# A fused attention and FP8 block on one core: later chunks prepared in pairs at other places, and entries' keys copied ahead of the divisions

## The chip, the cores and the metric

The kernel runs on one core of one Trainium2 chip. The metric is the device time of one execution in microseconds (us). The engines are TensorE (PE, matrix multiplication; PEld its weight loads), VectorE (DVE), ScalarE (ACT), GpSimd (POOL) and SyncE (SP), which here does nothing but issue DMAs. Each engine works through its own list of instructions in order and waits on semaphores for what others have to finish first.

## The reference, cut to what matters

The input `x` has 4 rows of 1024 tokens with 512 features. It is layer-normalized, and then three things are added: `x` itself, an attention layer, and a product with FP8-rounded operands.

```python
xn = layernorm(x)
out = x + attention(xn) + fp8_matmul(xn, input2)

# attention, per batch row, 16 heads of 128
q   = rope(rmsnorm(xn @ Wq + bq))
w   = softmax over groups of 4 tokens of (xn @ Wcmp + bcmp)
entries = sum over each group of w * xn          # 256 entries a row
ck  = rope(rmsnorm(entries @ Wk + bk)); cv = entries @ Wv + bv
sc  = q . ck, causal; the best 8 entries, softmax over them, times cv
lk  = rope(rmsnorm(xn @ Wlk + blk));  lv = xn @ Wlv + blv
local = softmax(q . lk over this and the previous 128 tokens) @ lv
attention = (sparse + local) / 2 @ Wo + bo
```

## The kernel before

**Chunks and units.** The tokens are cut into `NT` = 32 chunks of 128, eight to a batch row, numbered `t` = 0 to 31. A chunk has `NU` = 8 units `u`, each of two heads: unit `n` is `8 t + u`. One loop (L1012) goes over the units. In step `s` it issues, for several units at once, the pieces of a software pipeline: scores and softmax of unit `s`, queries of `s + 3`, normalization of the queries and keys of `s + 2`, values of `s - 1`, context and output of `s - 2`. The order in which these calls stand in the loop is the order on every engine; nothing reorders them.

For unit `s`, TensorE makes the scores (L750 for the previous 128 tokens, L757 for its own, L760 for the entries, out of `ckT`). `weigh` (L762) masks them and finds the best 8 on VectorE, then ScalarE takes the exponentials (L810, L818). `settle` (L821) removes what was not chosen and makes the reciprocals on VectorE, and `divide` (L838) multiplies on ScalarE (L843). `turn` (L854) transposes blocks of the probabilities on VectorE (L861), stores them to DRAM (`pr`, L869), and `fetch` (L898) brings them back transposed as `probT` (L903). `values` (L908), one step later, multiplies them with the values (L920). The first chunk and the last units do these transpositions on TensorE instead. The more entries there are, the wider the rows: chunks 1 to 3 of a batch row have three blocks of 128 a head, chunks 4 to 7 four.

**Preparing a later chunk.** `chunk_prep(t)` (L348) is a generator. It normalizes the tokens, transposes them by blocks on VectorE into `xb`, stores that to DRAM, and makes the weighted sums of four tokens, `few`, which lies in the same buffer as `xb`, and stores that to DRAM as `pooled`. The loop runs it on to a named step in given units (`FIRST_HALF`, `SECOND_HALF`, L991 to L992). A table `ready` (L998) says which chunks are prepared in which chunk. Where it names two, the second, `extra`, runs by `FIRST_HALF_MORE` and `SECOND_HALF_MORE` (L993 to L994) in units 2 to 5, and its `x` lies in a buffer of the tag `scratch`. That tag has two buffers; `xb` and the temporaries `qv` and `qm` of `chunk_eight` (L572, the FP8 part, which starts in unit 5 of every chunk) use it too.

The `pooled` store of chunks 0 to 7 is issued where the sums are made (L440); later ones are put into a list `stores`, which is issued near the end of a step (L1078), behind the fetches.

**Making entries.** `chunk_entries(g, n)` (L504) makes keys and values of entries from the pooled sums of the first `n` chunks of group `g` (`GC` = 4 chunks, 128 entries). A table `made` (L1000) says in which chunk this runs. It loads the sums in unit 4, multiplies on TensorE in unit 5 (L533, tile `ep`), normalizes and rotates on VectorE in units 5 and 6, and in unit 7 transposes the keys on TensorE (L568, tile `cp`) and copies them on ScalarE to `ckT` (L569). Unit 0 of the next chunk is the first to read them (L760). The generator is in the list `running`; `steps()` (L968) takes every generator there one step further, and is called twice in a step: once after `divide` and `turn` (L1052), once after the queries' squares (L1063). So the transposition and the copy of unit 7 stand at the first of these calls, behind the divisions on ScalarE.

## Time and profile before

| what | value |
|---|---|
| time, median of 3 runs | 2648.14 us (2648.01 to 2652.9) |
| the profiled execution's own time | 2649.72 us |
| its span, first to last instruction | 2647.9 us |
| mean granted TensorE clock | 0.999 of full speed |
| TensorE matmuls busy | 2607.9 us, 98% |
| VectorE busy | 2214.4 us, 84% |
| ScalarE busy | 1389.3 us, 52% |
| GpSimd busy | 783.9 us, 30% |
| DMA | 422.20 MB, 159 GB/s on the mean |

The page of the profile begins with the busy shares. Its second part cuts the span into 40 slices and gives each engine's busy share in tenths:

```profile
PE   8999999999999999999999999999999999999998
PEld 4666667676666666766766666666676666676776
DVE  6888888888888888888988888888888888877886
ACT  3545545555555555555555555555555555555554
```

The busy times of matmuls are modelled ends, so a digit 9 may still hold short waits. A list of waits names, for an engine, the line that waited, what ended its wait, the total time, how often, and the longest. A timeline gives start and duration of single instructions, or of several in a row that are alike, and in brackets the idle time before them with what ended it.

### The profile page before, as it was taken

The numbers are of one execution on the slowest core, as the hardware profiler recorded it, in microseconds if no ns is written. First come the engines' busy times: TensorE is split into PE (matmuls) and PEld (weight loads), VectorE is DVE, ScalarE is ACT, GpSimd is POOL, SyncE is SP. The second block draws the span as 40 slices with busy tenths as digits, with TensorE's granted clock in tenths as the row PEclk, the third lists the DMA queues.
The fourth block names the chain that finished last, engine by engine and source line by source line (L and its number), as shares of the span: only waits on it lengthen the run. The fifth ranks groups of instructions, "written<-read, shape, count | busy, mean of one in ns | idle before, by whom it ended". The sixth has DMA issues, their size and how long they took to land.

```text
span 2647.9 us, 46825 instructions
## 1 busy us (share of the span) xinstructions
PE 2607.9 (98%) x11844; PEld 1784.6 (67%) x11879; DVE 2214.4 (84%) x8381; ACT 1389.3 (52%) x5560; POOL 783.9 (30%) x1128
## 2 busy tenths in 40 slices
PE   8999999999999999999999999999999999999998
PEld 4666667676666666766766666666676666676776
DVE  6888888888888888888988888888888888877886
ACT  3545545555555555555555555555555555555554
POOL 3522333223332223232233222232323332322222
PEclk9999999999999999999999999999999999999999
DMA  8456556666655555666655556665665555566554
GB/s 252 113 155 160 149 139 177 178 166 161 165 142 157 158 150 162 165 175 175 162 156 147 155 148 159 172 165 159 174 180 144 149 147 152 150 167 172 158 152 111
DMA packets 722157, 422.20 MB, mean 159 GB/s; under 512 B 395728, under 2 KB 671457, under 8 KB 721889
## 3 DMA queue, kind: packets, MB, share of 16 engines
q1 hardware_dynamic: 721280, 418.80, 58.8%
q8 instruction: 97, 1.59, 0.3%
q14 instruction: 172, 1.40, 0.2%
q10 hardware_dynamic: 608, 0.41, 0.1%
HBM read 225.80 MB, written 193.20 MB: 158 GB/s over the span
## 4 chain that ended last, share of the span: by engine, by line
PE 83%; DVE 8%; ACT 3%; DMA 3%; SPq 1%; issue 1%; POOL 0%; DVEq 0%; ACTq 0%; POOLq 0%
PE qp L602 28%; PE op L953 14%; PE vp L708 14%; PE cp L920 13%; PE sc L760 5%; PE sc L757 4%; PE sc L750 4%; ACT prob L843 1%; ACT prob L810 1%; PE fp L584 1%; DVE sc L782 1%; DVE taken L808 1%; DVE probB L861 1%; PE ep L533 1%; ACT prob L818 1%
## 5 line engine op out<-in xcount | busy, mean ns | idle before, releaser
L602 PE MATMUL qp<-wqk,xnT 128*128 128x512 f32 x1552 | 711.0, 594 | 2.7 <-DMA wqk<-in_L_attn_Wlk_dram 2.7
L810 ACT ACTIVATE prob<-sc,neg 128x256 f32<-128x256 f32 (+1 forms) x512 | 235.6, 460 | 777.2 <-DVE taken L808 749.0
L602 PEld LDWEIGHTS qp<-wqk,xnT 128*128 128x128 f32 x1552 | 295.6, 191 | 372.2 <-issue 369.5
L843 ACT ACTIVATE prob<-prob,tot 128x256 f32<-128x256 f32 (+7 forms) x1024 | 382.0, 443 | 297.1 <-DVE tot L836 297.1
L708 PEld LDWEIGHTS vp<-wlv,xnT 128*128 128x128 f32 x2048 | 389.0, 190 | 161.2 <-issue 116.0
L953 PE MATMUL op<-wo,cT 128*128 128x512 f32 x1024 | 481.6, 593 | 2.8 <-ACT cT L935 2.8
L708 PE MATMUL vp<-wlv,xnT 128*128 128x256 f32 x2048 | 483.6, 379 | 0.0
L334 POOL TENSOR_TENSOR rb<-th,cs 128x256 f32<-128x256 f32 x256 | 203.3, 794 | 740.6 <-DVE th L630 733.6
L782 DVE CUSTOM_DVE_ANT_0 sc<-sc,mask_b 128x256 f32<-128x256 f32 (+1 forms) x512 | 211.5, 413 | 178.1 <-PE sc L760 168.0
L953 PEld LDWEIGHTS op<-wo,cT 128*128 128x128 f32 x1024 | 193.6, 190 | 228.4 <-issue 183.9
L861 DVE STREAM_TRANSPOSE probB<-prob 128x512 f32<-128x512 f32 (+2 forms) x490 | 305.7, 629 | 11.4 <-ACT prob L843 0.4
L312 POOL TENSOR_SCALAR r<-ss 128x4 f32<-128x4 f32 x256 | 61.0, 238 | 846.4 <-ACT junk L318 843.7
L920 PE MATMUL cp<-probT,lv 128*128 128x128 f32 x1920 | 298.7, 275 | 6.6 <-DMA probT<-pr 5.4
L318 ACT ACTIVATE junk<-qp 128x128 bf16<-128x128 f32 x1024 | 278.0, 272 | 29.7 <-PE qp L610 5.3
L920 PEld LDWEIGHTS cp<-probT,lv 128*128 128x128 f32 x1920 | 273.1, 191 | 24.7 <-issue 11.7
L630 DVE SCALAR_TENSOR_TENSOR th<-qp,r,norm_w 128x128 f32<-128x128 f32 x1024 | 286.1, 342 | 1.9 <-POOL r L313 1.6
L313 POOL TENSOR_TENSOR r<-r,nhalf 128x4 f32<-128x4 f32 x256 | 265.3, 1037 | 21.3
L826 DVE SCALAR_TENSOR_TENSOR prob<-taken,prob 128x128 f32<-128x128 bf16 (+7 forms) x512 | 187.2, 366 | 97.4 <-ACT prob L818 93.5
L602 PE MATMUL qp<-wqk,xone 128*128 128x512 f32 x496 | 258.3, 602 | 1.2 <-DMA xone<-xb_dram 1.2
L920 PE MATMUL cp<-probT,cv 128*128 128x128 f32 x1536 | 255.1, 275 | 0.0
L760 PE MATMUL sc<-ckT,qT 128*128 128x96 f32 (+7 forms) x1024 | 226.7, 303 | 6.9 <-ACT ckT L569 6.9
L920 PEld LDWEIGHTS cp<-probT,cv 128*128 128x128 f32 x1536 | 212.7, 192 | 0.0
(141 smaller groups left out, 3663.3 us busy)
## 6 DMA issues: line engine op xcount, KB each, us to landing
pr<-probB SPq DMA_DIRECT2D x125, 512.0 KB
probT<-pr SPq DMA_DIRECT2D x500, 128.0 KB
qk<-thb SPq DMA_DIRECT2D x992, 64.0 KB
pr<-probB SPq DMA_DIRECT2D x96, 384.0 KB
probT<-pr SPq DMA_DIRECT2D x384, 96.0 KB
qT<-qk SPq DMA_DIRECT2D x248, 128.0 KB
lkT<-qk SPq DMA_DIRECT2D x248, 128.0 KB
x_norm<-_attn_hidden_states_dram SPq DMA_DIRECT2D x32, 256.0 KB
```

Source lines behind the costliest of these rows:

```text
L313: nc.gpsimd.tensor_tensor(r, r, nhalf[: ss.shape[0], 0:n], ALU.pow)
L318: nc.scalar.activation(junk[: src.shape[0]], src, AF.Square, accum_out=acc)
L602: nc.tensor.matmul(qp, xnT[:, k, :] if k or not t else xone, wqk_sb[u][:, k, :], start=(k == 0), stop=(t > 0 and k == KK - 1),)
L630: nc.vector.scalar_tensor_tensor(th[:, i, :], qp[:, ts(i, D)], r[:, i : i + 1], norm_w[:, i // 2, :], ALU.mult, ALU.mult,)
L708: nc.tensor.matmul(vp[:, 0:256], xnT[:, k, :], wlv_sb[u][:, k, :], start=(k == 0), stop=(k == KK - 1),)
L760: nc.tensor.matmul(sc[:, spa], q, ckT[:, 0:m], start=True, stop=True)
L782: nc.vector.tensor_tensor_reduce(sc[h][:, loc], sc[h][:, loc], mask_b[:, loc], -1.0, TAKEN, ALU.add, ALU.min, neg[h][0],)
L810: nc.scalar.activation(probs[h][:, loc], sc[h][:, loc], AF.Exp, bias=neg[h][0], scale=-1.0, accum_out=tot[:, h, 0:1],)
L843: nc.scalar.mul(probs[h][:, cols], probs[h][:, cols], tot[:, h, part : part + 1])
L861: nc.vector.transpose(pb[:, :, ds(h * g, g), :], prob[:, parts[0] * P : (parts[-1] + 1) * P].rearrange("p (g b i) -> p b g i", b=NB, i=BLK),)
L920: nc.tensor.matmul(blocks(cp[:, h, :]), v, probT[:, :, h * len(parts) + i - parts[0], :], start=(i == parts[0]), stop=(i == parts[-1]),)
L953: nc.tensor.matmul(op, cT[:, h, :], wo_sb[u][:, h, :], start=(u == 0 and h == 0), stop=(u == NU - 1 and h == 1),)
```

## The change

It has three parts.

- `ready` and `made` change. Two chunks are prepared in chunks 2, 4 and 6 instead of 1, 2 and 3: chunk 1 prepares chunk 2, chunk 2 the chunks 3 and 4, chunk 3 chunk 5, chunk 4 the chunks 6 and 7, chunk 5 chunk 8, chunk 6 the chunks 9 and 10, chunk 7 chunk 11. From chunk 8 on nothing changes. The number of chunks with two stays three. Entries are made in chunks 0, 1, 2, 3 and 5 of the first batch row instead of 0, 1, 2, 3 and 4, and in chunk 3 from two chunks of the group instead of three; those in chunk 7 and later stay.
- The `pooled` store of chunks 8 to 11 is issued where the sums are made, too.
- In unit 7 of a chunk that makes entries, the generator is taken out of `running`. Its transposition is issued behind `queries` of that step, and its copy to `ckT` behind `settle` and ahead of `divide`. No instruction of TensorE lies between the old and the new place of the transposition, so only ScalarE's order changes: the copy comes ahead of the four divisions.

```diff
@@ chunk_prep
-        if t < 2 * GC:
+        if t < 3 * GC:
             nc.sync.dma_start(pooled[g][i], few)
         else:
             stores.append((pooled[g][i], few))
@@ chunk_entries
         nc.tensor.transpose(cp[:, 0:P], ck[:, 0, :], ident)
+        yield "turned"
         nc.scalar.copy(ckT[:, ts(half, P)], cp[:, 0:P])
         yield "A7"
@@ the tables
-    ready = {-1: [0], 0: [1], 1: [2, 3], 2: [4, 5], 3: [6, 7]}
-    ready.update({t: [t + GC] for t in range(GC, NT - GC)})
-    made = {0: (0, 2), 1: (0, 3), 2: (0, GC), 3: (1, 3), 4: (1, GC)}
+    ready = {-1: [0], 0: [1], 1: [2], 2: [3, 4], 3: [5], 4: [6, 7], 5: [8], 6: [9, 10], 7: [11]}
+    ready.update({t: [t + GC] for t in range(2 * GC, NT - GC)})
+    made = {0: (0, 2), 1: (0, 3), 2: (0, GC), 3: (1, 2), 5: (1, GC)}
     made.update({t: ((t + 1) // GC, GC) for t in range(2 * GC - 1, NT - 1, GC)})
@@ the loop over units
         for_unit(s + 3, (queries,))
+        if u == 7 and t in made:
+            running.remove(begun)
+            until(begun, "turned")
         if s < 0:
...
         for_unit(s, (settle,))
+        if u == 7 and t in made:
+            until(begun, "A7")
         for_unit(s, (divide,))
```

## The prediction, made before the changed kernel was run

> **What bounds the kernel.** I read first the page's busy shares: TensorE 98%, VectorE 84%, ScalarE 52%. So only TensorE's stalls can be won or lost. Then I cut the span at the first own-chunk score matmul (L757) of each chunk, from TensorE's timeline, and asked for busy times by these stretches. Chunks are numbered from 0, eight to a batch row; those below are 1 to 7, then 10, 11, 12 and 14.

> ```profile
> core 0: us, PE busy (x) PEld busy (x) DVE busy (x) ACT busy (x) POOL busy (x), PEclk, DMA share, GB/s
> 117.47:202.44 84.97, 81.06 (x362) 54.12 (x362) 70.72 (x278) 39.44 (x167) 27.12 (x39) 1.00 0.54 144
> 202.44:288.21 85.77, 81.40 (x366) 54.73 (x366) 70.55 (x283) 43.12 (x178) 25.18 (x42) 1.00 0.57 151
> 288.21:374.49 86.28, 81.63 (x367) 54.80 (x366) 71.14 (x279) 43.95 (x178) 25.13 (x40) 1.00 0.57 149
> 374.49:460.18 85.69, 83.84 (x395) 58.66 (x394) 73.00 (x273) 46.52 (x181) 24.54 (x38) 1.00 0.63 166
> 460.18:543.13 82.95, 82.90 (x389) 57.86 (x389) 71.89 (x261) 44.07 (x172) 23.78 (x33) 1.00 0.64 171
> 543.13:627.21 84.08, 83.99 (x389) 58.62 (x389) 74.07 (x261) 44.71 (x172) 24.29 (x33) 1.00 0.63 168
> 627.21:713.95 86.74, 86.69 (x396) 60.51 (x396) 75.53 (x264) 45.24 (x172) 25.71 (x36) 1.00 0.65 167
> ...
> 864.17:942.10 77.93, 77.88 (x357) 52.85 (x357) 64.85 (x260) 41.87 (x171) 22.26 (x33) 1.00 0.56 155
> 942.10:1021.99 79.89, 79.84 (x367) 54.85 (x366) 66.34 (x265) 42.87 (x174) 23.82 (x36) 1.00 0.57 155
> 1021.99:1103.63 81.64, 81.59 (x386) 56.55 (x385) 70.48 (x262) 43.92 (x174) 23.22 (x33) 1.00 0.63 170
> ...
> 1186.58:1271.22 84.64, 84.00 (x390) 58.65 (x389) 73.91 (x260) 44.53 (x172) 24.33 (x33) 1.00 0.63 167
> ```

> The first column is the length of the stretch. Chunks 10, 11 and 12 do what 2, 3 and 4 do, but prepare one later chunk each and (11 alone) make entries: there TensorE idles 0.05 us. They are my rows for a clean chunk. Making entries costs 11 against 10 only 1.95 us, of which 1.85 are the ep matmuls in unit 5. Chunks 1 to 3, which prepare two and make entries, lose 4 to 5 us each. The waits of VectorE and TensorE in chunks 1 to 3 say how:

> ```profile
> DVE qm_x L285 <- DMA pooled<-xb: 9.8, 3, 3.5
> DVE xb L375 <- DMA pooled<-xb: 7.9, 3, 2.7
> ...
> PE cp L920 <- DMA probT<-pr: 4.5, 5, 1.2
> PE sc L760 <- ACT ckT L569: 2.9, 2, 1.6
> ```

> (Columns: total us, times, longest.) Each pair stops VectorE twice, on the two buffers of the tag `scratch`: in unit 3 the second chunk's xb needs the buffer of the first until its pooled store has landed, in unit 5 chunk_eight's qm needs that of the second. VectorE's timeline of chunk 2 has both:

> ```profile
> 244.17 0.65 DVE L429 TENSOR_REDUCE xb<-x_norm 128x128 f32<-128x512 f32 x1
> ...
> 247.88 0.71 DVE L375 STREAM_TRANSPOSE xb<-x_norm 128x512 f32<-128x512 f32 x1 [2.61 <-DMA pooled<-xb]
> ...
> 271.74 0.43 DVE L285 TENSOR_SCALAR qm_x<-qv_x 128x512 uint32<-128x512 uint32 x1 [3.36 <-DMA pooled<-xb]
> ```

> **How a pair becomes TensorE time.** weigh (L782) starts at 235.40 in unit 3 of chunk 2 and at 272.54 in unit 6: 37.14 us for three units. Three clean units of chunk 10 take 3 x 9.635 = 28.90, so VectorE falls 8.24 behind. TensorE's ep matmuls fill 1.85 of it. The rest, 6.39, reaches TensorE through turn, its store and fetch, values. From the end of turn (L861) to the first L920 a clean unit of chunk 10 has 9.22 us; where it waited, in unit 6 of chunk 2 (turn ended 279.66, L920 began 286.56), the path took 6.90. So 2.32 are free, and TensorE should lose 6.39 - 2.32 = 4.07. It lost 85.77 - 79.89 - 1.85 (ckT wait, below) = 4.03. Chunk 3 likewise: L782 at 321.14 and 358.58, 0.22 late already, so 8.75 - 1.85 - 2.1 = 4.8; it lost 86.28 - 79.89 - 1.58 = 4.8. The rule holds twice.

> **The change, part by part.**

> *Chunk 1 loses its pair.* Units 0 and 1 keep their 10.43 and 10.80 (the lag there comes from chunk 0); units 2 to 7 become those of chunk 11 (9.64, 9.63, 9.64, 11.48, 9.64, 9.74): 81.0 instead of 84.97, **-3.97**. *Chunk 2* keeps pair and entries, but its unit 0 no longer waits: 12.34 becomes chunk 10's 10.49, **-1.85**. *Chunk 3 loses its pair*: 79.89 as chunk 11; the lag that chunk 2 hands over is late next, by about 0.2 in unit 0 (turn's end 13.24 + 6.90 against 19.97 us): **-6.2**.

> *Chunk 4* gives up entries and its unit-0 wait, and takes a pair. No ep matmuls fill the hole now. VectorE's idle time in units 3 to 5 is 6.3 in chunk 10 and 5.85 in chunk 12 (sums of the timeline), so it falls 8.24 + 0.45 = 8.7 behind. The path has 9.09 in a clean unit here; with four blocks a head the last fetch took up to 3.0 to land where L920 waited on it, so I take 7.2 for the path: 1.9 free. 8.7 - 1.9 = 6.8; 81.64 + 6.8 against 85.69: **+2.75**. *Chunk 5* takes the entries: **+1.95**, SP's five loads in unit 4 included, as in chunk 11. *Chunk 6* takes a pair: idle in units 3 to 5 of chunk 14 is 4.9, so 8.24 + 1.4 = 9.65 behind, 8.74 - 7.2 = 1.5 free, 8.15 lost; 83.81 (its units at 10.37, unit 0 at 11.23) + 8.15 against 84.08: **+7.9**. *Chunk 7* starts with this lag and has 1.2 to 1.5 us free a unit: **+0.4**.

> The bounds of a pair without entries: below, what a pair cost with them (4.0 in chunk 4, 4.8 in 6); above, no idle time of VectorE can be used any more and the stops (5.9) and its extra work (1.9 + 2.55 + 0.65 in units 3, 4, 5) count in full: 11.0 behind, 9.1 and 9.5 lost. I take the middle values, since idle time in the chunk differs by 0.45 and 1.4 us from the row, not by 6.

> *The store at L438* for chunks 8 to 11 goes ahead of the fetch. SP waits there for the reduction, 0.65 us after turn_keys, and issues 0.4 us; the fetch behind it waits anyway about 2.7 us for the pr store. Nothing; if that cover were gone, 0.5 us against at least 1.4 us free, so still nothing.

> *The early copy.* L569 is moved ahead of the divisions of unit 7. The order on TensorE stays (queries, transposition, to_output). ScalarE in chunk 7:

> ```profile
> 710.73 0.48 ACT L818 ACTIVATE prob<-sc,neg 128x256 f32<-128x256 f32 x1
> 713.18 1.71 ACT L843 ACTIVATE prob<-prob,tot 128x256 f32<-128x256 f32 x4 [1.97 <-DVE tot L836]
> 714.79 0.24 ACT L569 COPY ckT<-cp 128x128 f32<-128x128 f32 x1
> ```

> The transposition ran at 708.61 to 708.88, before the exponentials ended (711.21); so the copy fits into the 1.97 us before the divisions. [...] What goes is the wait of L760: 0.73 in chunks 8, 16 and 24 (2.2 in all; the others are counted above). Late next is probT: 8.01 - 0.73 = 7.28 against 7.2, just in time. I take **-2.0**.

> [...] The rows: store issued 246.19, VectorE on at 247.88, so 1.69 (332.10 to 333.79 the same). [...]

> **Sum:** -3.97 - 1.85 - 6.2 + 2.75 + 1.95 + 7.9 + 0.4 - 2.0 = **-1.0 us**. Span 2647.9 becomes 2646.9; the profiled run took 2649.72, 1.8 more than its span and 1.6 over the median, which the change does not touch. On the median of 2648.14: **2647.1**.

> **Rivals.**
> *A pair costs in chunks 4 and 6 what it cost in 2 and 3* (4.0 and 4.8). For it: these are the measured losses, and ep's absence also relieves SP (pr of unit 4 was issued at once in chunk 12, but 1.4 us after turn in chunk 2). Against it: VectorE's deficit does not depend on ep. Then -1.0 - 2.8 - 3.35 = -7.1: 2641.0.
> *The wider pr store lengthens the stops.* In chunks 4 and 6 pr has 512 KB instead of 384, and the pooled store stands behind it in SP's queue. 128 KB at the page's mean of 159 GB/s are 0.8 us, and the four issues of qk before it spread from 1.8 to 2.8 us: up to 1.8 a stop. All of a stop reaches TensorE, 4 x 1.8 = 7.2: 2654.3, slower. It decides from 1.6 us a stop. Against it: clean fetches after 512 KB start 2.8 us after turn, after 384 KB 2.6.
> *The early copy does not take effect*, as probT is late instead: +2.0, 2649.1, inside no change.

> **How the numbers follow.** A measurement of this kernel can tell 0.2%, 5.3 us, from no change. Forecast and third rival 0.61, first rival 0.26, second 0.13. The forecast's own range is 2643.5 to 2650.5 (the two pairs ±3, chance waits of clean units 0.6 each). Out to both rivals, less a tenth at each end: 2640.5 to 2652.5. Faster by over 0.2%: 0.26; within: 0.61; slower: 0.13.

> **What would show it.** Right: chunk 1 near 81, chunk 3 near 80, chunk 4 near 88.4, chunk 6 near 92; VectorE waiting for pooled six times, about 6 us a pair, now in chunks 2, 4 and 6; no wait of L760 for L569. Wrong: chunks 4 and 6 at 85.6 and 88.6 (first rival), stops over 4 us (second), divisions later after the end of the exponentials in unit 7 (the copy held them).

## The result, and the profile after

The changed kernel takes 2653.59 us (median of 21 runs, 2650.27 to 2658.85) beside 2650.02 of the kernel before on the same chips (21 runs, 2645.56 to 2654.44). The ratio is 1.0014, with a 95% interval of 1.0008 to 1.0020: slower by 3.7 us. The forecast was 1.0 us faster, 2647.1, and the range ended at 2652.5. Of the 6.5 us between the forecast and this, 1.9 lie in the median of the kernel before, which was 2648.14 over three runs and is 2650.02 over 21; the other 4.6 are the change's own.

The busy times of the changed kernel, cut at the first L757 (now L758) of each chunk, show chunks 1 to 7. The columns are those of the prediction's first view; lines after L568 have moved on by one.

```profile
119.23:200.10 80.87, 80.28 (x363) 54.37 (x362) 68.58 (x271) 41.95 (x175) 26.27 (x37) 1.00 0.54 145
200.10:283.56 83.46, 81.39 (x367) 54.72 (x366) 67.57 (x273) 40.84 (x170) 24.75 (x39) 1.00 0.59 155
283.56:363.71 80.15, 80.12 (x368) 54.76 (x366) 68.67 (x272) 45.16 (x180) 24.59 (x39) 1.00 0.56 152
363.71:454.12 90.41, 83.94 (x386) 56.97 (x385) 75.88 (x279) 45.41 (x182) 24.75 (x38) 0.99 0.62 161
454.12:539.75 85.63, 85.63 (x398) 60.58 (x398) 71.89 (x263) 43.87 (x170) 24.40 (x35) 0.99 0.65 168
539.75:633.74 93.99, 87.53 (x391) 59.59 (x389) 79.71 (x278) 46.87 (x180) 25.71 (x38) 0.98 0.60 157
633.74:720.13 86.39, 86.39 (x397) 60.67 (x396) 74.66 (x262) 44.59 (x169) 25.57 (x35) 1.00 0.63 167
```

| stretch | before | forecast step | measured step |
|---|---|---|---|
| chunk 1 | 84.97 | -3.97 | -4.10 |
| chunk 2 | 85.77 | -1.85 | -2.31 |
| chunk 3 | 86.28 | -6.2 | -6.13 |
| chunk 4 | 85.69 | +2.75 | +4.72 |
| chunk 5 | 82.95 | +1.95 | +2.68 |
| chunk 6 | 84.08 | +7.9 | +9.91 |
| chunk 7 | 86.74 | +0.4 | -0.35 |
| chunks 8, 16, 24 | 218.2 | -2.0 | -1.2 |
| sum | | -1.0 | +3.2 |

Chunks 4 and 6, where the pairs went, hold 4.0 of the 4.2 us by which the sum misses the forecast. The granted clock (the column before the last two) is below 1.00 in chunks 4 to 6; in the prediction's first view it is 1.00 in every stretch. Between these +3.2 and the span's +4.0 lie two things that are not traced to the change: the start, up to chunk 1, is 1.76 us longer (119.23 against 117.47), and the other later chunks are together 1.0 shorter.

VectorE's and TensorE's waits between 119 and 634 us:

```profile
DVE xb L375 <- DMA pooled<-xb: 8.3, 3, 2.9
DVE qm_x L285 <- DMA pooled<-xb: 8.1, 3, 2.8
```
```profile
PE cp L921 <- DMA probT<-pr: 9.2, 7, 3.1
PE op L954 <- ACT cT L936: 4.6, 7, 1.6
PE qp L603 <- DMA xone<-xb_dram: 0.8, 2, 0.5
```

The six stops of VectorE are where they were expected, and in sum no longer than before (16.4 us; before, 7.9 and 9.8). L760's wait for the copy is gone from the list. TensorE's wait for probT has doubled (4.5 us before, in chunks 1 to 3 alone), and its longest is 3.1 us. Its timeline at the end of chunk 4, with start, duration and the idle time in brackets, shows that wait and something behind it:

```profile
446.11 1.89 PE L709 MATMUL vp<-wlv,xnT 128*128 128x256 f32 x8
451.14 0.68 PE L921 MATMUL cp<-probT,lv 128*128 128x128 f32 x4 [3.14 <-DMA probT<-pr]
451.66 0.61 PE L921 MATMUL cp<-probT,cv 128*128 128x128 f32 x4
452.10 0.94 PE L921 MATMUL cp<-probT,lv 128*128 128x128 f32 x4
452.84 1.06 PE L921 MATMUL cp<-probT,cv 128*128 128x128 f32 x4
453.69 0.63 PE L751 MATMUL sc<-lkT,qT 128*128 128x128 f32 x2
```

Groups of four matmuls that took 0.61 us take 0.94 and 1.06 from 452.1 on. The clock of that place, by stretches of the changed kernel:

```profile
444.10:451.10 7.00, 3.71 (x12) 2.20 (x12) 6.32 (x26) 2.18 (x9) 4.83 (x8) 1.00 0.93 222
451.10:456.00 4.90, 4.86 (x27) 4.89 (x28) 3.78 (x9) 4.21 (x17) 1.43 (x4) 0.65 0.35 123
456.00:460.00 4.00, 4.00 (x13) 1.82 (x12) 3.44 (x16) 0.52 (x3) 1.25 (x2) 1.00 0.67 184
```

A mean of 0.65 over 4.9 us is 3.4 us at half speed and the rest at full: 1.7 us of matmul time are lost after the wait has ended. The clock records of the trace have the stretch itself, 452.22 to 455.63 us, and a second one at the end of chunk 6, 629.71 to 633.12. There the wait ends at 630.28, and the mean over the 4.9 us from 630.3 is 0.71: 1.4 us are lost.

### The profile page after: what moved, and what is told of

It is laid out like the page before. It is cut to its first block, busy times and chain, and to the rows that moved or that the text cites. A ratio compares the mean times of both kernels' runs of the same rounds, so it can differ in the third digit from the quotient of the medians.

```text
span 2651.9 us, 46860 instructions
## 1 busy us (share of the span) xinstructions
PE 2614.4 (99%) x11879; PEld 1786.5 (67%) x11879; DVE 2214.0 (83%) x8381; ACT 1392.2 (52%) x5560; POOL 785.3 (30%) x1128
## 3 DMA queue, kind: packets, MB, share of 16 engines
q8 instruction: 97, 1.59, 0.3%
## 4 chain that ended last, share of the span: by engine, by line
PE 86%; DVE 6%; DMA 3%; SPq 2%; ACT 2%; issue 1%; POOL 0%; DVEq 0%; ACTq 0%; POOLq 0%
PE qp L603 29%; PE op L954 15%; PE vp L709 14%; PE cp L921 13%; PE sc L761 5%; PE sc L758 4%; PE sc L751 4%; PE fp L585 1%; DMA probT<-pr 1%; PE ep L533 1%; DVE probB L862 1%; SPq L692 1%; ACT prob L811 1%; DVE sc L783 1%; DVE wqk L269 1%
## 5 line engine op out<-in xcount | busy, mean ns | idle before, releaser
L783 DVE CUSTOM_DVE_ANT_0 sc<-sc,mask_b 128x256 f32<-128x256 f32 (+1 forms) x512 | 211.7, 414 | 181.0 <-PE sc L761 171.0
L921 PE MATMUL cp<-probT,lv 128*128 128x128 f32 x1920 | 300.3, 276 | 12.0 <-DMA probT<-pr 10.4
L921 PEld LDWEIGHTS cp<-probT,lv 128*128 128x128 f32 x1920 | 273.7, 192 | 31.7 <-issue 16.0
L921 PE MATMUL cp<-probT,cv 128*128 128x128 f32 x1536 | 256.1, 276 | 0.0
L921 PEld LDWEIGHTS cp<-probT,cv 128*128 128x128 f32 x1536 | 213.7, 193 | 0.0
```

The source lines that it names most:

```text
L783: nc.vector.tensor_tensor_reduce(sc[h][:, loc], sc[h][:, loc], mask_b[:, loc], -1.0, TAKEN, ALU.add, ALU.min, neg[h][0],)
L921: nc.tensor.matmul(blocks(cp[:, h, :]), v, probT[:, :, h * len(parts) + i - parts[0], :], start=(i == parts[0]), stop=(i == parts[-1]),)
```

## The experiments

The theory after the result: the tables cost the time, the early copy pays a little; VectorE's two stops a pair are the root, they reach TensorE one for one, and a wait that grows to some 3 us costs TensorE's clock as well. Rivals: the early copy holds ScalarE; VectorE has no room for a second chunk late in a row, stops or not; the slow matmuls come from something else. Each kernel was timed in several rounds beside the kernel before.

### The copy alone, and the tables alone

`copy_only` is the kernel before with the third part of the change (`yield "turned"` and the two `if u == 7 and t in made` of the loop). `tables_only` is the changed kernel without it.

> The kernel before with the early copy alone, tables unchanged. Theory (the moved pairs cost the time, the copy pays a little): unit 0 of chunks 2, 3 and 4 loses its wait for the copy, some 1.3 to 1.8 us each, chunks 8, 16 and 24 together 1.2 as in the changed kernel: -5 us in all, ratio 0.998; divisions not later. Rival (the early copy holds ScalarE and the divisions behind it): no gain or a loss, ratio 1.000 to 1.002.

> The changed kernel with the copy put back behind the divisions. Theory: the loss in chunks 4 and 6 stays (about +9 each with the unit after), chunk 3 gets its wait of 1.3 us back and chunks 8, 16 and 24 their 1.2: 2.5 us slower than the changed kernel, ratio to before 1.0023. Rival (the copy costs): faster than the changed kernel, ratio below 1.001.

Measured: copy alone 0.9990 [0.9981, 0.9999], tables alone 1.0032 [1.0021, 1.0044]. So the copy gains and the tables lose, and the rival falls. ScalarE of `copy_only` in unit 7 of chunk 7:

```profile
707.07 0.48 ACT L819 ACTIVATE prob<-sc,neg 128x256 f32<-128x256 f32 x1
707.43 0.28 ACT L570 COPY ckT<-cp 128x128 f32<-128x128 f32 x1
709.52 1.71 ACT L844 ACTIVATE prob<-prob,tot 128x256 f32<-128x256 f32 x4 [1.81 <-DVE tot L837]
```

The copy fills the gap, and VectorE's reciprocals still set the divisions. The gain of the copy alone is half of what I expected, 2.7 us and not 5: behind a pair the next wait stands close. In chunk 4 unit 0 became 1.90 us shorter, and unit 1 lost 0.97 of it, 0.74 in a wait for probT. Tables alone came out 2.4 us worse than I expected. Its trace has L760's wait back four times, 3.1 us in all, so the copy's gain is of the size seen in the changed kernel; the rest of the difference is about the width of the interval.

### A filler in the long waits

```diff
         for_unit(s + 1, (values_of,))
+        if u == 7 and t in (4, 6):
+            for _ in range(12):
+                nc.tensor.matmul(
+                    units[s + 1]["vp"][:, 256:512], bias_b[:, 0:P], bias_b[:, 0:256],
+                    start=True, stop=True,
+                )
```

> The changed kernel with 12 short bf16 matmuls of no use ahead of L921 in unit 7 of chunks 4 and 6, some 1.6 us within the waits of 3.1 and 2.7 us; they write columns of vp that nobody reads. Theory (the long wait lets the granted clock fall, 0.75 and 0.79 in the 7 us behind it): the clock stays at 1.00, L921 and the scores behind it take their usual 0.61 and 0.40, chunks 4 and 6 with the unit after them are 1.4 us shorter each, 2.8 in all, ratio to before about 1.0003. Rival (the slow matmuls come from something else, such as the DMAs that land at that time): they stay slow, no change, 1.0014.

Measured: 1.0007 [0.9998, 1.0016]. The intervals of this and of the changed kernel overlap, so the ratios alone do not settle it; the trace does. TensorE of `after_fill` at the end of chunk 4:

```profile
445.77 1.47 PE L1077 MATMUL vp<-bias_b 128*128 128x256 bf16 x12
448.82 0.68 PE L921 MATMUL cp<-probT,lv 128*128 128x128 f32 x4 [1.58 <-DMA probT<-pr]
449.34 0.61 PE L921 MATMUL cp<-probT,cv 128*128 128x128 f32 x4
449.79 0.61 PE L921 MATMUL cp<-probT,lv 128*128 128x128 f32 x4
450.23 0.61 PE L921 MATMUL cp<-probT,cv 128*128 128x128 f32 x4
```

The wait for probT ends no earlier, since VectorE is as late as before; but of its 3.1 us only 1.58 are idle, the matmuls behind it keep their 0.61, and the clock of the 4.9 us from 448.8 is 1.00. Units 7 of chunks 4 and 6 are 1.14 and 1.24 us shorter than in the changed kernel, and unit 0 of chunk 5 another 0.71. Of chunk 6 as a whole only 0.24 is won, since its unit 4 took 1.01 longer there, behind a wait of 1.75 us for cT. Whether the filler or the place of the wait kept the clock up is worked out in the last section: the filler in chunk 4, not in chunk 6. DMAs land at that time in both kernels (DMA share 0.35 in the changed kernel's 4.9 us from 451.1, 0.37 in these); the clock is what differs.

The timed executions point the same way. Each has a mean granted clock on record. It averages 0.9974 over the 21 of the changed kernel, 0.9985 over the 11 of `after_fill`, and 0.9985 and 0.9983 over the 22 and 25 of the kernel before beside which the experiments were timed. A clock lower by 0.0009 to 0.0011 over 2650 us is 2.4 to 2.9 us (an estimate), most of the 3.7 us by which the changed kernel is slower; it counts half-speed stretches in the start, too.

### Without the stops

```diff
-    def chunk_prep(t):
+    def chunk_prep(t, pair=False):
...
         few = xb[:, 0:P]
+        if pair:
+            few = work.tile([P, KK * P], BF16, tag="x8", name=f"few_{t}", bufs=1)
+            few = few.bitcast(F32)[:, 0:P]
```

With `pair` set for both chunks of a pair (`after_few`), for the first only (`after_first`) or for the second only (`after_second`), the pooled store reads the buffer of `x8`, which chunk_eight needs only at its end. `xb` is free as soon as the sums are made.

> The changed kernel with the sums of a pair written into the buffer of x8, not into xb, so that xb is free before the store of pooled has landed. Theory (VectorE's two stops a pair, 5.3 us, are what TensorE pays): no stop is left; chunk 4 with the unit after 7 us shorter, chunk 6 7 to 8, chunk 2 1.5 to 2.5; 16 us in all, ratio to before about 0.995. Rival (VectorE has no room for the work of a second chunk, 5.1 us, so late in a batch row): the stops go, but chunks 4 and 6 stay over 4 us above 81.6 and 83.8; at most 8 us gained, ratio 0.998 to 1.000.

> The changed kernel with only the first chunk's sums of a pair in the buffer of x8: the stop in unit 3 (2.7 us a pair) goes, that in unit 5 stays. Theory (what VectorE is behind reaches TensorE one for one, and the clock falls only after a long wait): VectorE 2.7 less behind, so chunks 4 and 6 with the unit after some 2.7 + 1.4 (clock) shorter each, chunk 2 one, 9 in all: ratio 0.998. Rival (the two stops overlap with idle time that VectorE has anyway, and only both together cost): under 3 us gained, ratio above 1.000.

> The changed kernel with only the second chunk's sums of a pair in the buffer of x8: the stop in unit 5 (2.7 us a pair) goes, that in unit 3 stays. Theory: the same 9 us as without the first stop, ratio 0.998, and TensorE's wait in unit 7 of chunks 4 and 6 under 1 us. Rival: under 3 us gained.

| kernel | ratio to before | chunk 2 | chunk 4 and unit after | chunk 6 |
|---|---|---|---|---|
| changed | 1.0014 [1.0008, 1.0020] | 83.46 | 90.41 + 11.83 | 93.99 |
| `after_first` | 0.9984 [0.9975, 0.9993] | 83.18 | 87.65 + 11.45 | 90.10 |
| `after_second` | 0.9976 [0.9966, 0.9986] | 81.82 | 86.72 + 11.13 | 89.92 |
| `after_few` | 0.9958 [0.9944, 0.9971] | 82.24 | 83.41 + 11.12 | 87.32 |

Chunks 4 and 6 of `after_few`, by stretches:

```profile
359.69:443.11 83.42, 82.56 (x386) 56.25 (x385) 74.95 (x276) 44.21 (x175) 24.53 (x37) 1.00 0.67 174
528.01:615.33 87.32, 84.92 (x390) 58.31 (x389) 78.97 (x276) 45.80 (x175) 25.49 (x37) 1.00 0.66 169
```

VectorE's work is the same (74.95 beside 75.88 us in chunk 4), its waits for pooled are gone, and TensorE gets 7.0 us back in chunk 4, 0.7 in the unit after, and 6.7 in chunk 6. So VectorE has room for the second chunk's work; it had none for the stops. The rival falls for chunk 4, where 1.8 us are left over the clean 81.64; in chunk 6 3.5 are left over 83.81, so there part of it holds. Each stop alone is worth 3 to 4.5 us in chunks 4 and 6, as the theory has it. Part of that is the clock: it fell behind chunk 4 of `after_first`, but not behind chunk 6 there, nor behind 4 and 6 of `after_second`. Without its 1.7 us in chunk 4 and 1.4 in chunk 6, in those three, a stop of 2.7 is worth 2.5 to 3.1. Without the first stop the second grows (9.6 us for three, after 8.1), which takes some of that gain back.

### The second GpSimd operation later

```diff
         nc.gpsimd.tensor_tensor(v, v, m, ALU.add)
         yield
+        if tag in ("x_4", "x_6"):
+            yield
```

> The changed kernel with the second GpSimd operation of chunk_eight (L291) one call of steps later in chunks 4 and 6, so that it is behind the queries' statistics. Theory (L836 of unit 6 takes 1.11 instead of 0.17 us because L291 runs at that time): L836 of unit 6 takes 0.17, turn ends 0.9 earlier, and chunks 4 and 6 are 0.9 shorter each, if the operations moved into unit 7 hold nobody: 1.8 us, ratio 1.0007. Rival (L836 waits for something else, such as ScalarE's accumulator): it stays at 1.11, no change.

This asks for a wait in unit 6 that the prediction had left out. In the changed kernel the small operation L836, with which the reciprocals begin, lasts 1.11 us there, while GpSimd does L291. Timelines of VectorE and of GpSimd in the changed kernel:

```profile
439.28 1.11 DVE L836 TENSOR_SCALAR tot<-tot 128x4 f32<-128x4 f32 x1
440.43 0.18 DVE L837 RECIPROCAL tot<-tot 128x4 f32<-128x4 f32 x1
```
```profile
439.02 1.35 POOL L291 TENSOR_TENSOR qv_x<-qv_x,qm_x 128x512 f32<-128x512 f32 x1
```

The two end together, at 440.39 and 440.37. With the `yield`, VectorE has at the same place (L836 is L838 there):

```profile
439.35 0.17 DVE L838 TENSOR_SCALAR tot<-tot 128x4 f32<-128x4 f32 x1
```

So the reason is shown. The time is not won: 1.0016 [1.0007, 1.0025]. Chunk 4 was 2.03 us shorter, of which some 1.1 are the clock, which did not fall there, and 0.9 the yield. But the operations moved into later units held VectorE there: it waited 2.99 us at 455.77 for x8's last operation, and unit 1 of chunk 5 lost 1.81. Chunk 6 gained 0.35, and chunk 7 lost 1.44.

### The old places without stops

`copy_few` is the kernel before with the early copy and with `few` in the buffer of x8 for both chunks of a pair, in chunks 1, 2 and 3.

> The kernel before with the early copy and with the sums of a pair in the buffer of x8; pairs in chunks 1, 2 and 3 as before. Theory (the stops are the price of a pair, wherever it stands): chunks 1, 2 and 3 keep some 2.4 us each, as chunk 2 does with the changed tables and no stops; about as fast as the changed kernel without stops, ratio 0.995 to 0.997. Rival (early in the row a pair is much cheaper, since VectorE has more idle time and ep fills the hole): under 1 us a pair left, ratio 0.994 or less.

Measured: 0.9962 [0.9948, 0.9975]. Chunks 1, 2 and 3 take 84.04, 82.08 and 82.15. Without a pair they take 80.87 (chunk 1 of the changed kernel) and 79.89 (chunk 11, for 2 and 3), so a pair without stops costs 2.2 to 3.2 us here, as the theory has it, beside 1.8 and 3.5 in chunks 4 and 6. This and `after_few` beat both kernels of the study, and cannot be told from each other. Without the stops it does not matter much where the pairs stand.

## Why the prediction was wrong

**What held.** Where the time goes was read rightly: chunks 1, 2 and 3 gain 12.5 us (12.0 forecast), the entries in chunk 5 cost 1.97 once the clock's 0.71 is taken off (1.95 forecast), the early copy delays no division, the stops last what they lasted, so the wider store lengthens none of them (the second rival falls). The first rival falls too: in chunks 4 and 6 a pair costs twice what it cost with ep, and without the clock's 1.7 and 1.4 still 7.8 and 8.8 us. The copy gains 1.2 in chunks 8, 16 and 24, not 2.0, since probT is late next.

**The steps that failed** are those of chunks 4 and 6, "6.8 lost" and "8.15 lost". Measured over the clean 81.64 and 83.81, with the 0.71 that the clock cost in unit 0 of chunk 5, the loss is 9.5 and 10.2. Term by term:

| term | chunk 4 forecast | measured | chunk 6 forecast | measured |
|---|---|---|---|---|
| VectorE behind, unit 3 to 6 | 8.7 | 7.7 | 9.65 | 8.4 |
| more from weigh to turn in unit 6 | 0 | 1.1 | 0 | 1.0 |
| free: clean path less waiting path | 1.9 | 9.09 - 7.95 = 1.1 | 1.5 | 8.74 - 7.60 = 1.1 |
| half-speed clock | 0 | 1.7 | 0 | 1.4 |
| loss | 6.8 | 9.4 | 8.15 | 9.7 |

(VectorE behind: in chunk 4 L783 starts at 396.13 in unit 3 and 434.31 in unit 6, 38.18 less 30.46 for three clean units. Weigh to turn's end in unit 6: 8.88 against 7.74 in a clean unit 5; the L836 row is 0.94 of it. Path: turn's end 443.19, L921 451.14.)

The rule by which VectorE's lag becomes TensorE's wait held a third and fourth time. Its first term was taken 1.0 and 1.2 us too large, mostly because the stop of unit 5 is 2.64 and not 3.36 in chunk 4. Three things were missing. First, I took the free time from a unit whose L836 takes 0.17; where no entries are made, L291 falls on L836 in unit 6, in the clean chunks too (in chunk 12 of before the operation, L835 there, takes 1.11 us at 1089.76, and L291 runs from 1089.50 to 1090.84), and I had seen that in none of the chunks that I took the rule from, since all of them make entries. Second, the path through the DMAs took 0.4 to 0.75 us more than the 7.2 assumed (7.95 and 7.60; the DMA engines were 93% busy from 444.1 to 451.1 us, 76% from 622.3 to 630.3). Third, and the largest, the clock. My sum added waits as if TensorE went on at full speed behind each of them. In the trace of before the waits stay under 1.9 us after the first 30 us, and the clock stays at 1.00 in every stretch of the prediction's first view. But the start of that trace, ahead of the first view, has two stretches at half speed, 9.94 to 13.36 and 54.32 to 57.73 us, and the forecast itself made waits of over 2 us. I did not ask what such a wait does; what the runs show of it is in the last section. The clock's 3.1 us, put at nothing, are most of the miss: the errors of the other terms nearly cancel, to 0.9 us in chunk 4 and 0.2 in chunk 6, and that they do is luck. In chunk 6 0.5 us more are in no term.

**What stays open:** `tables_only` is 8.5 us slower by its ratio, but chunks 1 to 7 of its one profile show 4.0, with one half-speed stretch in them. In that profile the rest lies in the start, where both kernels do the same work: chunk 1 begins at 121.32 us and not at 117.47, 3.85 later. The six timed executions are ordered by their mean clock, from 2652.46 us at 0.999 to 2661.77 at 0.995. So a good part of the excess goes with the clock; how much of it is the tables' doing, six executions do not settle.

## What to carry to other kernels

In this kernel, with one engine 98% busy, a lag of another cost it nothing until the slack of the path between them was used up, and from there one for one (the terms above add up to 9.4 of 9.5 us in chunk 4 and 9.7 of 10.2 in chunk 6); so a burst of work that stops its engine was cheaper where the busy engine had work of its own to fill the hole. (A pair with stops cost 4.0 and 4.8 us beside the ep matmuls, 7.8 and 8.8 without them, though those chunks have longer rows, too.) Before moving a burst, ask what makes it long: here two waits, of 2.6 to 2.9 us each in the changed kernel, for a buffer whose store had not landed, and another buffer for 64 KB of sums was worth 15 us at the new places (ratio 1.0014 to 0.9958) and 7 at the old (0.9990 to 0.9962), more than any place in the order. The waits of 2.6 to 3.1 us on the busy engine had a second price here: behind five of the seven the clock was at 0.50 for 3.4 us, which cost 1.7 and 1.4 us in the changed kernel, and a sum of wait lengths leaves that out.

## What the runs showed of the hardware

```profile
448.81:452.22 3.41, 1.08 (x10) 1.11 (x11) 2.94 (x8) 1.58 (x5) 1.96 (x3) 1.00 0.78 141
452.22:455.63 3.41, 3.41 (x18) 3.41 (x17) 2.76 (x6) 3.09 (x14) 1.06 (x3) 0.50 0.39 154
626.30:629.71 3.41, 1.30 (x7) 0.79 (x5) 2.94 (x13) 1.70 (x6) 2.17 (x4) 1.00 0.86 195
629.71:633.12 3.41, 2.84 (x13) 2.87 (x14) 3.21 (x7) 2.26 (x6) 1.01 (x2) 0.50 0.27 48
```

This table has the waits for probT at the end of chunks 4 and 6, TensorE's busy time in the emptiest window that the wait touches, and the clock of the window after that one:

| kernel, chunk | wait | busy of 3.41 us | clock of the next window |
|---|---|---|---|
| changed, 4 | 3.14 | 1.08 | 0.50 |
| `after_first`, 6 | 2.92 | 1.53 | 1.00 |
| `tables_only`, 4 | 2.76 | 1.04 | 0.50 |
| changed, 6 | 2.69 | 1.30 | 0.50 |
| `tables_only`, 6 | 2.67 | 1.59 | 1.00 |
| `after_yield`, 6 | 2.65 | 0.77 | 0.50 |
| `after_first`, 4 | 2.61 | 0.80 | 0.50 |
| `after_yield`, 4 | 2.40 | 1.84 | 1.00 |
| `after_fill`, 4 | 1.58 | 2.45 | 1.00 |

The length of the wait does not decide: the 2.92 us of `after_first` fell across two windows and left 1.53 us of matmuls in the emptier one. From 60 to 2600 us the ten traces have some 7400 such windows. The five with 1.30 us of matmuls or less were followed by half speed, and none of the others, all with 1.53 or more, was. Where between 1.30 and 1.53 the limit lies, no window shows. By the same count, without the filler the emptiest window of `after_fill` would have held some 1.1 us in chunk 4 and 1.6 in chunk 6 (estimates from its rows). So, by this count, in chunk 4 the filler kept the clock up; in chunk 6 the place of the windows would have done it alone.

In the first 60 us busy time alone does not decide: windows with 1.8 us of matmuls were followed by half speed in four traces and by full speed in others, for a reason not found. Unit 2 of chunk 0 takes 14.1 us in these four and 12.4 in the others, which is one half-speed stretch, and chunk 1 begins anywhere from 115.85 to 121.32 us. So single profiles of kernels as close as these must not be compared by their spans.
